# Block products seeded in PSUM, and two sums by accumulating DMA, in a cross-attention kernel

## The chip, the core and the metric

The kernel runs on one core of a Trainium2 chip. The core has TensorE (PE: matrix products into the accumulators in PSUM, with a weight load ahead of each that overlaps the product before), VectorE (DVE), ScalarE (ACT), GpSimd (POOL) and the queue of SyncE (SP). Transfers are issued by SP, ACT and POOL and carried by 16 DMA engines. Everything is fp32. The time is the device time of one launch in microseconds, the median of several runs.

## The reference

There are eight batches. For each, `x1` and `x2` are 512 x 1024:

```python
q = jnp.einsum('bcn,dc->bnd', x1, Wq) + bq
k = jnp.einsum('bcn,dc->bdn', x2, Wk) + bk[:, None]
v = jnp.einsum('bcn,dc->bdn', x2, Wv) + bv[:, None]
attn = jax.nn.softmax(jnp.einsum('bnd,bdm->bnm', q, k), axis=2)
attn_out = jnp.einsum('bcm,bnm->bcn', v, attn)
return attn_out + x1
```

with 64 rows in `Wq` and `Wk` and 512 in `Wv`.

## The kernel before

The values are not formed. For each batch the kernel computes y = x2 · E, where E holds the exponentials of the scores (1024 x 1024, keys by queries), scales the columns of y by the reciprocal sums, and then computes Wv · y, to which the bias and x1 are added. The first product is called stage "y", the second stage "o".

**Seven products instead of eight.** Both stages split their operands into 2 x 2 quarters ("11", "12", "21", "22") and use seven quarter products with sums of quarters: S1 to S4 on the left, T1 to T4 on the right. The table `MULT` names the operands of each product and the PSUM bank it goes to: products 1, 6, 5, 3 run on in the banks a0 and a1 (two halves j of 128 rows), products 2, 7, 4 in c0 and c1. Between products 1, 6 and 5 the running sum is copied out by ScalarE (L332) to tiles u1, u6, u5 in SBUF, and VectorE adds such a copy to bank c when a quarter of the result is evicted (`evict_y`, L502, `evict_o`, L548): `RESULT` says which copy goes with which quarter. The quarter "12" is bank a at the end, with no copy.

**A second level.** A quarter product of stage y is 8 matmuls of 128 x 128 by 128 x 512, or it is done "in blocks": its operands are split once more (`inner_left`, four sums of 128 x 256 each at L355; `inner_right`, four sums of 128 x 512 each at L367), and seven block products of two matmuls of 256 columns follow (`inner_product`, L374). Their partial products lie in PSUM tiles of the pool `ps_s`; ScalarE copies them to SBUF tiles d and v (L383), and VectorE adds those to the copies u or to the bank's content. Batch 0 has products 3 and 4 in blocks, batches 1 and 6 products 2, 3 and 4, batches 2 to 5 and 7 products 2, 3, 4 and 7 (`seven`, L712). Product 2 has a routine of its own, `multiply_2` (L388), with six VectorE additions (L418); `multiply_7` (L464) adds its d to u5 and u6 (L471).

**Sums.** S1, S2, S4 are VectorE additions of 128 x 1024 (`sum_a`, L110), S3 too, in place of "21". T1, T2, T3 are VectorE subtractions (`sum_e`, L262), T3 in place of "12". From batch 2 on, T4 is made by two ScalarE copies (L278) and two accumulating transfers (L280), issued by GpSimd.

**The order of work.** The order of each engine's queue is the order of the program text; only waits are added. `period` (L708) writes out one batch `s`, with the next batch `n` woven in: products 1, 2, 6 of y; scores of the first half of the queries of `n` (L191, copied by ScalarE, L200 and L198); the queries of the batch after it; products 5, 7, 3; scores of the second half; keys of the batch after; product 4; then stage o in the order 1, 6, 2, 5, 7, 3, 4. GpSimd finds the maxima and the sums over partitions by all-reduce (`highest` L221, `total` L226), issues the small transfers that turn a sum into a row of reciprocals (`shares`), adds up the exponentials by accumulating transfers (L555), and adds x1 to the results likewise (L551). SP loads `a` (x2 transposed, L133) and `x` (L126) and stores the results (L552).

Around the change in stage o stand these lines:

```python
        second(7)
        if s.b and n:
            sum_a(n, "S1", "S2")
        evict_o(s, "22")
        ...
            sum_a(n, "S3")
            inner_left(n, 2, n.a["12"], "aS4")
            inner_right(n, 2, n.e[0][:, 1], "eT4")
            second(3)
            evict_o(s, "12")
            second(4)
            evict_o(s, "21")
```

Tiles are named by tags, and a tag with one buffer makes a new tile wait for all uses of the old one. yT1, yT2 and yT4 hold T1, T2 and T4 of stage o, and lend themselves to sums of blocks in stage y; u1, y11, y12, y22, i2, aS4, eT1, eT2 likewise have several users.

## Time and profile before

| | |
|---|---|
| runs, median (lowest to highest of 3) | 690.9 us (690.63 to 691.11) |
| profiled execution, span from first to last instruction | 689.5 us |
| granted TensorE clock, mean | 0.999 |
| period of batch 3 (288.16 to 371.82) | 83.66 us; PE 83.66, DVE 80.06, ACT 35.64, POOL 24.72 busy; DMA share 0.67 |
| period of batch 7 (617.0 to 689.5) | 72.50 us; PE 68.82, DVE 59.73, ACT 15.69, POOL 9.42 busy; DMA share 0.46 |
| DMA queues | GpSimd's (q0) 36.25 MB, 30.1% of 16 engines' span; SP's (q1) 70.13 MB, 29.4% |
| T4's accumulating transfers | 12 of 512 KB, 6.8 us from issue to landing (median; 5.3 to 8.3) |

A row of the groups reads: line, engine, operation, output and inputs by the program's names, shapes, count, busy time in all, mean ns of one, and the idle time before with what ended it. Some rows that bear on the change:

```profile
L332 ACT COPY uy<-ps_ya 128x512 f32<-128x512 f32 x48 | 28.0, 586 | 138.9 <-PE ps_ya L321 124.9
L383 ACT COPY d<-ps_i 128x256 f32<-128x256 f32 x84 | 29.3, 374 | 47.6 <-PE ps_i L374 47.0
L548 DVE SCALAR_TENSOR_TENSOR uo<-ps_oc,bv_sb,uo 128x512 f32<-128x512 f32 x42 | 29.5, 741 | 1.6 <-PE ps_oc L321 1.6
```

A matmul of the program is two instructions in the profile, and matmuls overlap, so the mean of one is longer than the time it adds; the chain of waits shows what a group adds.

### The profile page before, as it was taken

To read this page: it belongs to the slowest core of one execution; us is meant where nothing else is said; L and a number is where in the kernel's file an instruction comes from. 1 tells how busy PE (TensorE), PEld (TensorE's weight loads), DVE (VectorE), ACT (ScalarE), POOL (GpSimd) and SP (SyncE) were. 2 spreads that over 40 slices of the span, in tenths; PEclk is the share of its full clock that TensorE was granted. 3 is DMA by queue.
4 is the path that set the end of the run, shared out by engine and by line. 5 is a ranking of instruction groups with operands and counts; after the bars stand their busy time and mean duration, and the time that the engine had idled before them with its cause. 6 is when DMAs were issued, how large, how long until landed. Compare 5 with 4: busy or idle time off the path is not lost.

```text
span 689.5 us, 6656 instructions
## 1 busy us (share of the span) xinstructions
PE 683.1 (99%) x2252; PEld 365.3 (53%) x2252; DVE 630.4 (91%) x809; ACT 275.7 (40%) x439; POOL 189.3 (27%) x147
## 2 busy tenths in 40 slices
PE   9999999999999999999999999999999999999997
PEld 5333554535545465455654566454754545545763
DVE  1999999988999889998999989999899988999894
ACT  2734263146233562435533454324544245333220
POOL 0124113521423123231232321423223241324100
PEclk9999999999999999999999999999999999999999
DMA  9666266954558854696638867298642874259403
GB/s 301 263 218 231 70 183 120 252 162 92 184 106 208 236 100 160 129 243 182 125 130 160 241 176 166 69 187 224 181 81 41 185 200 77 62 108 248 102 0 123
DMA packets 44723, 109.05 MB, mean 158 GB/s; under 512 B 4880, under 2 KB 7184, under 8 KB 44688
## 3 DMA queue, kind: packets, MB, share of 16 engines
q0 software_dynamic: 17424, 36.25, 30.1%
q1 hardware_dynamic: 25856, 70.13, 29.4%
q10 hardware_dynamic: 1408, 2.23, 1.1%
q8 instruction: 18, 0.29, 0.2%
q14 instruction: 17, 0.14, 0.1%
HBM read 72.62 MB, written 16.81 MB: 130 GB/s over the span
## 4 chain that ended last, share of the span: by engine, by line
PE 94%; DMA 3%; SPq 1%; ACT 1%; DVE 1%; issue 0%; DVEq 0%
PE ps_ya L321 24%; PE ps_i L374 17%; PE ps_oa L321 16%; PE ps_oc L321 12%; PE ps_s L191 6%; PE ps_yc L374 5%; PE ps_q L149 4%; PE ps_k L149 3%; PE ps_ya L374 3%; PE ps_yc L321 3%; DMA a<-in_x2T_dram 1%; DMA x_in_x_dram<-in_x_dram 1%; DMA x_head<-in_x_dram 1%; PE ps_sc L191 1%; PE ps_sa L191 1%; DVE aS L110 0%
## 5 line engine op out<-in xcount | busy, mean ns | idle before, releaser
L321 PE MATMUL ps_ya<-eT,aS 128*128 128x512 f32 x256 | 113.1, 595 | 0.0
L332 ACT COPY uy<-ps_ya 128x512 f32<-128x512 f32 x48 | 28.0, 586 | 138.9 <-PE ps_ya L321 124.9
L321 PEld LDWEIGHTS ps_ya<-eT,aS 128*128 128x128 f32 x256 | 48.0, 190 | 60.9 <-issue 58.8
L253 ACT ACTIVATE e<-e 128x1024 f32<-128x1024 f32 x60 | 63.0, 1059 | 42.3 <-DVE e L249 40.8
L249 DVE TENSOR_TENSOR e<-e,top 128x1024 f32<-128x1024 f32 x60 | 69.8, 1214 | 11.0 <-POOL top L221 11.0
L221 POOL PARTITION_ALL_REDUCE top<-max x16 | 32.8, 2052 | 154.6 <-DVE max L215 79.3
L226 POOL PARTITION_ALL_REDUCE den<-sum x16 | 59.2, 3701 | 40.8 <-DVE sum L215 35.8
L321 PE MATMUL ps_oa<-yT,w_S 128*128 128x512 f32 x128 | 57.6, 593 | 0.0
L321 PE MATMUL ps_oc<-y,w 128*128 128x512 f32 x128 | 57.6, 593 | 0.0
L321 PE MATMUL ps_ya<-e,a 128*128 128x512 f32 x128 | 56.3, 593 | 0.3 <-ACT e L244 0.3
L200 ACT COPY e<-ps_s 128x1024 f32<-128x1024 f32 x46 | 45.7, 1028 | 19.3 <-PE ps_s L191 18.1
L332 ACT COPY uo<-ps_oa 128x512 f32<-128x512 f32 x48 | 27.4, 583 | 53.0 <-PE ps_oa L321 41.3
L383 ACT COPY d<-ps_i 128x256 f32<-128x256 f32 x84 | 29.3, 374 | 47.6 <-PE ps_i L374 47.0
L551 POOL DMA_DIRECT2D uo<-in_x_dram x21 | 24.9, 1184 | 85.0 <-DVE uo L548 85.0
L191 PE MATMUL ps_s<-q,k 64*128 64x512 f32 x188 | 47.3, 608 | 0.8 <-ACT q L590 0.8
L555 POOL DMA_DIRECT2D sum<-e x21 | 25.7, 1222 | 66.5 <-DMA sum<-e 32.7
L321 PEld LDWEIGHTS ps_ya<-e,a 128*128 128x128 f32 x128 | 24.2, 190 | 31.3 <-issue 29.6
L321 PEld LDWEIGHTS ps_oa<-yT,w_S 128*128 128x128 f32 x128 | 24.2, 190 | 30.8 <-issue 29.9
L321 PEld LDWEIGHTS ps_oc<-y,w 128*128 128x128 f32 x128 | 24.0, 190 | 31.0 <-issue 28.5
L211 DVE TENSOR_TENSOR max<-max,e 128x1024 f32<-128x1024 f32 x30 | 36.7, 1225 | 3.0
L507 DVE TENSOR_TENSOR y<-y,den 128x512 f32<-128x512 f32 x54 | 33.7, 681 | 0.0
L548 DVE SCALAR_TENSOR_TENSOR uo<-ps_oc,bv_sb,uo 128x512 f32<-128x512 f32 x42 | 29.5, 741 | 1.6 <-PE ps_oc L321 1.6
(142 smaller groups left out, 1274.5 us busy)
## 6 DMA issues: line engine op xcount, KB each, us to landing
x_in_x_dram<-in_x_dram SPq DMA_DIRECT2D x60, 512.0 KB, 6.2
a<-in_x2T_dram SPq DMA_DIRECT2D x32, 512.0 KB, 6.3
sum<-e POOLq DMA_DIRECT2D x21, 512.0 KB, 5.1
uo<-in_x_dram POOLq DMA_DIRECT2D x21, 512.0 KB, 6.4
out_dram<-uo SPq DMA_DIRECT2D x21, 512.0 KB, 4.1
eT<-eT POOLq DMA_DIRECT2D x12, 512.0 KB, 6.8
den<-row POOLq DMA_DIRECT2D x16, 256.0 KB, 3.6
r<-in_x_dram POOLq DMA_DIRECT2D x7, 512.0 KB, 8.7
```

The costliest lines, as they stand in the source:

```text
L149: nc.tensor.matmul(ps[r, :], w_sb[:, c, :], s.x[:, c, ts(h, H)], start=(c == 0), stop=(c == CT - 1),)
L191: nc.tensor.matmul(ps[g], s.k[r, ts(i, P)], s.q[r, ts(h, H)], start=True, stop=True)
L200: nc.scalar.copy(e[:, :, i, :], whole)
L211: nc.vector.tensor_tensor(f, e[:, :, 0, :] if i == 1 else f, e[:, :, i, :], op)
L221: nc.gpsimd.partition_all_reduce(s.top[h], s.mx[h][:, 0, :], P, ReduceOp.max)
L226: nc.gpsimd.partition_all_reduce(s.den[h], s.mx[h][:, 0, :], P, ReduceOp.add)
L249: nc.vector.tensor_tensor(e, e, top, ALU.subtract)
L253: nc.scalar.activation(e, e, AF.Exp)
L321: nc.tensor.matmul(ps[:, n], left[ka][:, k, ts(j, P)], right[kb][:, k, n], start=opens and k == 0, stop=i in (2, 3, 4) and k == n_k - 1, s ...
L332: nc.scalar.copy(s.tmp[i][:, j, :], ps)
L374: nc.tensor.matmul(ps, s.inner[i][ka][:, k, :], s.inner[i, "t"][kb][:, k, :], start=opens and k == 0, stop=z in (2, 3, 4) and k == MH // 2 ...
L507: nc.vector.tensor_tensor(y[:, j, :], y[:, j, :], rden, ALU.mult)
```

## The change

In batches 2 to 7 (`late`) product 1 of y is done in blocks too, by a new routine `multiply_seeded`, which also takes over product 2 (batches 1 to 7) and product 7 (where it was in blocks). In this routine ScalarE copies a partial block product from the PSUM tile of `ps_s` to the place in bank a or c where it belongs, and later block products are accumulated onto it by matmuls there; one VectorE addition in PSUM (`complete`) follows. `multiply_2`, `inner_bank` and `multiply_7` go, and with them their additions. The blocks' sums for product 1 of the next batch are made in stage o, around the sums S1 and S2. The copies u1 of product 1 are made by hooks within product 2.

In stage o of all batches product 1 goes to a PSUM tile `both`, ScalarE copies it to a0 and a1, where product 6 runs on, and product 2 is accumulated onto `both`, which then is block 11 of the result; it is evicted by ScalarE with the bias (in the last batch by VectorE).

T3 of batches 2 to 7 is made by ScalarE, which negates "12", and accumulating transfers that add "22". S4 is loaded as "12" of x2 transposed and S2 is added by an accumulating transfer. Several sums of blocks move to other places in the order, and the scaling of y11, y22 and y12 with them.

```diff
+    def sum_t3(s, i):
+        t3 = s.t["T3"][:, i : i + 2, :]
+        nc.scalar.mul(t3, t3, -1.0)
+        nc.gpsimd.dma_start(t3, s.t["22"][:, i : i + 2, :], accum_op=ALU.add)
+
+    def sum_s4(s):
+        s.a["S4"] = sb.tile([P, MH, C // 2], F32, tag="aS4", name=f"aS4_{s.b}")
+        nc.sync.dma_start(s.a["S4"], x2T[s.b, 0, 1])
+        nc.gpsimd.dma_start(s.a["S4"], s.a["S2"], accum_op=ALU.add)
+
+    def copy_u1(s, j):
+        if j == 0:
+            s.tmp[1] = sb.tile([P, 2, H], F32, tag="u1", name=f"uy1_{s.b}")
+        nc.scalar.copy(s.tmp[1][:, j, :], s.bank["a", j])
...
+    def multiply_o1(s):
+        both = ps_s.tile([P, 2, H], F32, tag="sc", name=f"ps_o1_{s.b}")
+        for j in range(2):
+            s.bank["p", j] = ps = both[:, j, :]
+            for k in range(2):
+                nc.tensor.matmul(
+                    ps, w["11"][:, k, ts(j, P)], s.y["11"][:, k, :], start=k == 0, stop=False, skip_group_check=True
+                )
+            s.bank["a", j] = a = ps_a.tile([P, H], F32, tag=f"a{j}", name=f"ps_oa{j}_{s.b}_1")
+            nc.scalar.copy(a, ps)
...
+    def multiply_seeded(s, i, v_tag, hooks={}):
+        bank = MULT[i][2]
+        b0, b1 = (
+            ps_a.tile([P, H], F32, tag=f"{bank}{j}", name=f"ps_y{bank}{j}_{s.b}_{i}") for j in range(2)
+        )
+        s.bank[bank, 0], s.bank[bank, 1] = b0, b1
+        parts = ps_s.tile([P, 2, H], F32, tag="sc", name=f"ps_i{i}_{s.b}")
+        chain, third = parts[:, 0, left], parts[:, 1, left]
+        v = sb.tile([P, 2, H], F32, tag=v_tag, name=f"v{i}_{s.b}")[:, 0, left]
+        for z, ps, opens, out, of in (
+            (1, chain, True, b0[:, left], chain),
+            (7, third, True, v, third),
+            (6, chain, False, b1[:, left], chain),
+            (2, b0[:, left], False, None, None),
+            (5, chain, False, b0[:, right], chain),
+            (4, b1[:, left], False, b1[:, right], chain),
+            (3, b0[:, right], False, None, None),
         ):
+            inner_product(s, i, z, ps, opens)
+            if out is not None:
+                nc.scalar.copy(out, of)
+            if z in hooks:
+                hooks[z]()
+        def complete():
+            b = b1.rearrange("p (a n) -> p a n", a=2)
+            nc.vector.tensor_tensor(b, b, v.unsqueeze(1).to_broadcast([P, 2, H // 2]), ALU.add)
...
-        bank, add = RESULT[k]
+        bank, add = RESULT[k] if k != "11" else ("p", None)
...
-        seven = 2 <= s.b < B - 2 or n is None
+        late = s.b >= 2
+        seven = late and (s.b < B - 2 or n is None)
...
-        first(1)
+        if late:
+            complete_1 = multiply_seeded(s, 1, "y11")
...
+        if late:
+            shares(s, 0)
+            for i in range(1, MH):
+                fold(s, 1, i, "sum", ALU.add)
+            complete_1()
         sum_e(s, "T1", "T2")
-        if s.b < 2:
+        if late:
+            total(s, 1)
...
-            evict = multiply_2(s)
-            sums(s, 1)
-            evict()
+            complete_2 = multiply_seeded(
+                s, 2, "y22", {6: lambda: copy_u1(s, 0), 5: lambda: copy_u1(s, 1)} if late else {},
+            )
+            if late:
+                sum_t3(s, 0)
+                sum_t3(s, 2)
...
+            complete_2()
+            evict_y(s, "11", (1,))
...
             sum_t4(s)
-            sum_a(s, "S4")
-        sum_e(s, "T3")
+            if late:
+                sum_s4(s)
...
+        if late:
+            inner_left(s, 4, s.a["22"], "a12")
+            evict_y(s, "11", (2,))
...
         shares(s, 1)
         if seven:
+            inner_right(s, 7, s.t["T3"], "yT1", "yT2")
...
             first(5, (lambda: exponential(n, 0, 0)) if n else None)
+            inner_left(s, 3, s.a["S4"], "aI3")
             inner_right(s, 3, s.t["22"], "eT1")
-            inner_left(s, 4, s.a["22"], "a12")
-            add_7 = multiply_7(s, hooks[0])
-            add_7()
+            complete_7 = multiply_seeded(s, 7, "y12", hooks[0])
+            complete_7()
+            evict_y(s, "22", (1,))
             evict_3 = multiply_3(s, hooks[1])
-            evict_y(s, "22", (1,))
-            if n:
-                evict_3()
             inner_right(s, 4, s.t["T4"], "eT2")
-            if not n:
-                evict_3()
+            evict_y(s, "22", (2,))
+            evict_3()
+            evict_y(s, "12", (2,))
...
         if s.b and n:
+            inner_right(n, 1, n.e[0][:, 0], "yT1", "yT2")
             sum_a(n, "S1", "S2")
+            inner_left(n, 1, n.a["11"], "i2")
         evict_o(s, "22")
```

More of the change, by code (lines that the diff above doesn't have):

```diff
@@ L312, in multiply @@
         ka, kb, bank, opens = MULT[i]
+        if stage == "o" and i == 2:
+            bank, opens = "p", False
         for j in range(2):
@@ L383, in inner_product @@
             nc.scalar.copy(copy, ps)
-    def inner_bank(s, i, z):
-        return ps_s.tile([P, 2, H], F32, tag="sc", name=f"ps_i{i}{z}_{s.b}")[:, 0, left]
-    def multiply_2(s):
-        chain = ps_a.tile([P, H // 2], F32, tag="c0", name=f"ps_i20_{s.b}")
-        second = ps_a.tile([P, H // 2], F32, tag="c1", name=f"ps_i21_{s.b}")
-        third = inner_bank(s, 2, 2)
-        uv = sb.tile([P, 4, H // 2], F32, tag="i2", name=f"i2_{s.b}")
-        u, v = uv[:, 0:2], uv[:, 2:4]
-        for z, ps, opens, *copies in (
-            (1, chain, True, v[:, 0, :]),
-            (2, second, True),
-            (6, chain, False, u[:, 0, :]),
-            (7, third, True, v[:, 1, :]),
-            (5, chain, False, u[:, 1, :]),
-            (4, third, False),
-            (3, chain, False),
-        ):
-            inner_product(s, 2, z, ps, opens, *copies)
-        def evict():
-            u0, u1 = s.tmp[1][:, 0, :], s.tmp[1][:, 1, :]
-            s.y["11"] = y = sb.tile([P, 2, H], F32, tag="y11", name=f"y11_{s.b}")
-            for out, x, z in (
-                (u0[:, left], u0[:, left], v[:, 0, :]),
-                (y[:, 0, left], second, u0[:, left]),
-                (u1, u1, u.rearrange("p a n -> p (a n)")),
-                (y[:, 1, right], v[:, 1, :], u1[:, right]),
-                (y[:, 1, left], third, u1[:, left]),
-                (y[:, 0, right], chain, u0[:, right]),
-            ):
-                nc.vector.tensor_tensor(out, x, z, ALU.add)
-        return evict
@@ new lines, in multiply_seeded @@
+    def multiply_seeded(s, i, v_tag, hooks={}):
[15 more added lines that the diff above has]
+            (3, b0[:, right], False, None, None),
+        ):
+            inner_product(s, i, z, ps, opens)
[6 more added lines that the diff above has]
+            nc.vector.tensor_tensor(b, b, v.unsqueeze(1).to_broadcast([P, 2, H // 2]), ALU.add)
+        return complete
@@ L422, in multiply_onto @@
     def multiply_onto(s, i, d_tag, v_tag, hooks={}):
-        bank, opens = MULT[i][2:]
-        if opens:
-            for j in range(2):
-                s.bank[bank, j] = ps_a.tile([P, H], F32, tag=f"{bank}{j}", name=f"ps_y{bank}{j}_{s.b}_{i}")
+        bank = MULT[i][2]
         b0, b1 = (s.bank[bank, j] for j in range(2))
-        chain, third = inner_bank(s, i, 0), inner_bank(s, i, 2)
+        parts = ps_s.tile([P, 2, H], F32, tag="sc", name=f"ps_i{i}_{s.b}")
+        chain, third = parts[:, 0, left], parts[:, 1, left]
@@ L439, in multiply_onto @@
             6: (chain, False, d[:, 1, 0, :]),
-            2: (b0[:, left], opens),
+            2: (b0[:, left], False),
             5: (chain, False, d[:, 0, 1, :], d[:, 1, 1, :]),
-            4: (b1[:, left], opens),
+            4: (b1[:, left], False),
             3: (b0[:, right], False),
         }
-        for z in (1, 2, 7, 6, 4, 5, 3) if opens else (1, 7, 6, 2, 5, 4, 3):
+        for z in (1, 7, 6, 2, 5, 4, 3):
             inner_product(s, i, z, *steps[z])
@@ L462, in multiply_4 @@
             nc.vector.tensor_tensor(u6, u6, d[:, j, :], ALU.add)
-    def multiply_7(s, hooks):
-        d, complete = multiply_onto(s, 7, "i2", "y12", hooks)
-        def add():
-            complete()
-            for k in (5, 6):
-                nc.vector.tensor_tensor(s.tmp[k], s.tmp[k], d, ALU.add)
-        return add
     def multiply_3(s, hooks):
@@ L496, in evict_y @@
         y = s.y[k]
-        alone = 7 in s.inner and add in (5, 6)
         for step in steps:
@@ L500, in evict_y @@
                 if step == 1:
-                    ps, n = s.bank[bank, j], left if alone and j else slice(0, H)
-                    nc.vector.tensor_tensor(y[:, j, n], ps[:, n], s.tmp[add][:, j, n], ALU.add)
-                elif alone and j:
-                    for x, n in ((y, left), (s.tmp[add], right)):
-                        nc.vector.tensor_tensor(y[:, j, n], x[:, j, n], rden[:, n], ALU.mult)
+                    nc.vector.tensor_tensor(y[:, j, :], s.bank[bank, j], s.tmp[add][:, j, :], ALU.add)
                 else:
@@ L519, in bias @@
             return bv_sb[:, 2 * r + j : 2 * r + j + 1]
+        if s.b == B - 1 and k == "11":
+            o = s.x[:, 0:2, ts(h, H)]
+            for j in range(2):
+                nc.vector.scalar_tensor_tensor(
+                    o[:, j, :], s.bank[bank, j], bias(j), o[:, j, :], ALU.add, ALU.add
+                )
+                nc.sync.dma_start(out[s.b, ts(j, P), ts(h, H)], o[:, j, :])
+            return
         if s.b == B - 1 and add is None:
@@ L541, in evict_o @@
         if add is None:
-            o = sb.tile([P, 2, H], F32, tag="r", name=f"r_{s.b}")
+            o = sb.tile([P, 2, H], F32, tag="u1" if k == "11" else "r", name=f"r{k}_{s.b}")
             for j in range(2):
@@ L717, in second @@
         def second(i):
-            multiply(s, "o", i, w, s.y, 2, n is None and i == 3)
+            if i == 1:
+                multiply_o1(s)
+            else:
+                multiply(s, "o", i, w, s.y, 2, n is None and i == 3)
         open_t(s)
@@ L722, in period @@
             load_x(s, x1)
-        first(1)
+        if late:
+            complete_1 = multiply_seeded(s, 1, "y11")
+        else:
+            first(1)
         if s.b == 0:
             head_second(s, n)
+        if late:
[3 more added lines that the diff above has]
+            complete_1()
         sum_e(s, "T1", "T2")
-        if s.b < 2:
+        if late:
+            total(s, 1)
+        else:
             total(s, 0)
-        else:
-            shares(s, 0)
         if n:
@@ L740, in period @@
             shares(s, 0)
+            sum_e(s, "T3")
         else:
-            evict = multiply_2(s)
-            sums(s, 1)
-            evict()
+            complete_2 = multiply_seeded(
+                s,
+                2,
+                "y22",
+                {6: lambda: copy_u1(s, 0), 5: lambda: copy_u1(s, 1)} if late else {},
+            )
+            if late:
+                sum_t3(s, 0)
+                sum_t3(s, 2)
+            else:
+                sums(s, 1)
+            complete_2()
+            evict_y(s, "11", (1,))
             if s.b == 1:
@@ L747, in period @@
             sum_t4(s)
-            sum_a(s, "S4")
-        sum_e(s, "T3")
+            if late:
+                sum_s4(s)
+            else:
+                sum_a(s, "S4")
+                sum_e(s, "T3")
         if n:
@@ L754, in period @@
             inner_right(s, 4, s.t["T4"], "eT2")
-        if s.b:
             inner_left(s, 3, s.a["S4"], "aI3")
-        if s.b > 1 and not seven:
-            inner_left(s, 4, s.a["22"], "a12")
         if seven:
             inner_left(s, 7, s.a["S3"], "yT4")
-            inner_right(s, 7, s.t["T3"], "yT1", "yT2")
+        if late:
+            inner_left(s, 4, s.a["22"], "a12")
+            evict_y(s, "11", (2,))
         def add_exponential(i):
@@ L799, in period @@
             first(5, (lambda: exponential(n, 0, 0)) if n else None)
+            inner_left(s, 3, s.a["S4"], "aI3")
             inner_right(s, 3, s.t["22"], "eT1")
-            inner_left(s, 4, s.a["22"], "a12")
-            add_7 = multiply_7(s, hooks[0])
-            add_7()
+            complete_7 = multiply_seeded(s, 7, "y12", hooks[0])
+            complete_7()
+            evict_y(s, "22", (1,))
             evict_3 = multiply_3(s, hooks[1])
-            evict_y(s, "22", (1,))
-            if n:
-                evict_3()
             inner_right(s, 4, s.t["T4"], "eT2")
-            if not n:
-                evict_3()
+            evict_y(s, "22", (2,))
+            evict_3()
+            evict_y(s, "12", (2,))
         else:
@@ L820, in period @@
                 start_sum(n, 0)
+                if late:
+                    inner_left(s, 3, s.a["S4"], "aI3")
                 inner_right(s, 3, s.t["22"], "eT1")
@@ L831, in period @@
                 evict_y(s, "22", (1,))
-        for k in ("11", "12", "22"):
-            evict_y(s, k, (2,))
+            for k in ("12", "22") if late else ("11", "12", "22"):
+                evict_y(s, k, (2,))
         if s.b == 1:
```

## The prediction, made before the changed kernel ran

> Times called t count from the first product matmul of the fourth batch's period (288.16 us into the span), the steady state taken as the pattern. Periods are numbered by batch, 0 to 7.

> **What bounds it now.** I read the header, then the chain of waits, then a timeline of each engine over one period, then windows of 1.5 us for the DMA engines.

> ```profile
> span 689.5 us, 6656 instructions
> PE 683.1 (99%) x2252; PEld 365.3 (53%) x2252; DVE 630.4 (91%) x809; ACT 275.7 (40%) x439; POOL 189.3 (27%) x147
> PE 94%; DMA 3%; SPq 1%; ACT 1%; DVE 1%; issue 0%; DVEq 0%
> ```
> TensorE has no idle time to win back after the head; time can fall only by fewer matmul columns, and any wait put on TensorE shows in full. The chain prices a product:

> ```profile
> 288.16 6.87 PE ps_ya L321 x16
> 295.02 6.04 PE ps_i L374 x28
> ```
> A whole product of y takes 6.87 us (0.43 per instruction), one in seven blocks 6.04 (0.216 each, 0.863 per block product).

> VectorE is the second engine to know: its timeline in that period runs without gaps but for 1.83 us before the exponentials' subtraction and 0.49 us in product 3.

> ```profile
> 284.09 1.22 DVE L110 TENSOR_TENSOR a<-a,a 128x1024 f32<-128x1024 f32 x1
> 285.23 0.42 DVE L355 TENSOR_TENSOR aI<-a 128x256 f32<-128x256 f32 x1
> ...
> 286.69 0.68 DVE L367 TENSOR_TENSOR eI2eT<-e 128x512 f32<-128x512 f32 x1
> 287.41 0.69 DVE L367 TENSOR_TENSOR eI2eT<-eI2eT,e 128x512 f32<-128x512 f32 x1
> 288.02 0.68 DVE L367 TENSOR_TENSOR eI2eT<-e 128x512 f32<-128x512 f32 x1
> 288.62 0.68 DVE L367 TENSOR_TENSOR eI2eT<-e,eI2eT 128x512 f32<-128x512 f32 x1
> 289.22 1.40 DVE L548 SCALAR_TENSOR_TENSOR uo<-ps_oc,bv_sb,uo 128x512 f32<-128x512 f32 x2
> ```
> Start to start, four left sums take 1.46 us (285.23 to 286.69), four right sums 2.53 (to 289.22).

> **TensorE's work.** Product 1 of y goes into blocks for batches 2 to 7: 6 x (6.87 - 6.04) = **5.0 us less**. Products 2 and 7 were in blocks already where they are now; the block 11 of the result keeps its matmuls. So 690.9 - 5.0 = 685.9 is the floor. The sum is made against the span, 689.5; the 1.4 us outside it, up to the median of 690.9, are taken as unchanged.

> **ScalarE.** Per period: five block copies in product 1, one more in product 2 (L383: 0.372 us each), two negations for T3 (as L278's copy, 1.043), two bias copies for block 11 (L544: 0.687); 2.2 + 2.1 + 1.4 = 5.7 us on an engine that is busy 35.6 of 83.66 us. TensorE now waits for these copies: a block product that adds onto a copy comes one block product later, so 0.863 us covers 0.372 plus 0.04 from matmul end to copy start (the copies at L383 start so). No row has a copy that ends in PSUM. From below it costs no less than nothing of the end, being hidden; from above, at twice its row to SBUF (0.74), it still fits. Product 1 of the result: a 0.585 copy of the first half has the second half, 1.72 us, as cover. I take 0 for all of these. If ScalarE were late instead, as behind the wait of L332 for an output transfer (305.09, t = 16.9), about 1 us a period would be lost: the eviction of block 21 ends at t = 2.4 now and at about 3.3 then, its output goes out that much later, and the copies of the scores follow it, with 3 us to spare before and about 1 after.

> [...]

> **VectorE, in sum.** Per period it loses T3 (2.27 us), S4 (1.21 when undisturbed), two additions in product 7 (2.28), block 11's eviction (1.32) and trades product 2's eviction (2.6) for 1.9; it gains the right and left sums of product 1 (2.53 + 1.46) and one addition (0.65). About 3 us less in all, worth nothing by itself, since TensorE is the bound. What counts is order, at two places.

> **Place one: block 22's eviction in the result stage.** The sums for the next batch's product 1 are queued ahead of evict_o("22"). Their first writes tile yT1, which product 5 of the result reads until it ends; product 4 adds onto the bank that the eviction reads. In between TensorE has products 7 and 3: 6.87 us, or 6.69 from product 5's last end to product 4's first start (277.84 to 284.53). VectorE in that time: right sums 2.53, S1 and S2 2.39 (280.38 to 282.77), left sums 1.46, first half of the eviction 0.74: 7.12 us, plus 0.06 to start and 0.13 to the matmul. TensorE waits 7.31 - 6.69 = **0.62 us** in batches 2 to 5, where VectorE arrives about 1 us before product 5 ends. In batch 1 it arrives 0.25 late by its timeline (0.85 us), in batch 6 some 0.6 late, without the keys' cover (1.2 us). Sum 4 x 0.62 + 0.85 + 1.2 = **4.5 us lost**: nearly all of the gain. Bounds: 3 to 7.

> **Place two: T3 and S4 come by DMA.** Each period adds two transfers of 512 KB for T3, a load and an accumulation of 512 KB for S4. GpSimd issues them in the order T3, T3, T4, T4, S4 after the all-reduce of the denominators (3.18 us, now from about t = 13.3), at some 1.1 us each: T3 from t = 17.4, S4 at 21.7. Ahead of them on the engines are an output and now four loads, not three. Rows of the windows (engine times, clock, DMA share, GB/s at the end):

> ```profile
> 309.00:310.50 1.50, 1.50 (x8) 0.60 (x8) 1.47 (x5) 1.39 (x2) 0.00 (x0) 1.00 1.03 214
> 310.50:312.00 1.50, 1.50 (x10) 0.41 (x8) 1.47 (x5) 1.50 (x4) 0.00 (x0) 1.00 1.10 216
> 312.00:313.50 1.50, 1.50 (x10) 0.56 (x8) 1.50 (x3) 0.93 (x2) 0.00 (x0) 1.00 0.99 197
> 313.50:315.00 1.50, 1.50 (x8) 0.29 (x4) 1.45 (x2) 0.00 (x0) 0.00 (x0) 1.00 0.23 44
> ...
> 316.50:318.00 1.50, 1.50 (x5) 0.74 (x4) 1.47 (x2) 0.09 (x1) 0.00 (x0) 1.00 0.97 328
> ```
> T4's two accumulations run at 209 GB/s with the engines full: 1.05 MB in 5.0 us. They end at 313.5 (t = 25.3); the four loads of x that follow the queries' matmuls take 316.5 to 324 at 298 GB/s, 7.0 us for 2.1 MB. So the engines are full from before T4 to t = 36, but for 2.6 us. After the change T3 stands in T4's place and lands, behind one more load (1.8 us at 298 GB/s), at t = 27; T4 and S4's accumulation, 7.5 us of engine time, then meet the loads of x, 7.0 us, from the same t = 27. S4 lands at 34.5 if GpSimd's queue goes first, at 41.5 if SP's does. No row has both queues deep at once; I take the middle, **38**.

> [...]

> What waits for S4: product 3 of y in blocks. Its second block product, nominally at t = 40.15, needs left sums (1.46), three right sums (1.93) and 0.13: S4 by 36.6. At 38 TensorE waits 1.4 us. VectorE is held meanwhile with the completion of product 7, block 22, the right sums of product 4 and block 12 behind it, 8.3 us from there to the bank that the next scores' third pair needs, which TensorE reaches in 7.1: another 1.2. So **2.6 us a period** (0 to 6.1) in batches 2 to 5: **10.4 us** (0 to 24). Batch 6 has no load of x then, and a whole product 7 as cover: 0. Batch 7 has no scores and no queries between its products: product 7 starts at t = 25.8, its second block product at 26.7 needs three right sums after T3's landing at 27: 2.3 us; S4 at 34.5 holds product 3 by 38 - 35 = 3: **5 us** (0 to 8). GpSimd's small transfers for the shares stand behind S4 too; the shares are needed only after the sums that S4 holds, so 0.

> T3 itself in batches 2 to 5: its sums come before the subtraction that the exponentials need, which moves from 1.83 us of waiting to about 1 us of slack. A landing at 27 costs nothing, one after 28.5 would hold TensorE through ScalarE's queue.

> **Sum:** 690.9 - 5.0 + 4.5 + 10.4 + 5 = 705.8, so **706 us**; with each bound at its end 689 to 725, of which I keep 688 to 718.

> **Rivals.** (1) The transfers keep up: S4 before t = 36.6, as it would with GpSimd's queue served first (34.5). For it: the engines' share over the period is only 0.67. Against it: the windows above. Time 690.9 - 5.0 + 4.5 + 1 = 691.4, **not slower** in a measurable way. Chance 0.18. (2) The vector queue isn't the limit at block 22 either, because product 1's right sums start before product 5 ends or the sums overlap more; this decides from 0.6 us less VectorE time there. For it: VectorE has 3 us less to do. Against it: the tile yT1 and the order in the code. Time 685.9 to 688.5, **faster**. Chance 0.15. (3) The change doesn't do what it says: a ScalarE copy into PSUM takes over 0.82 us and every block chain waits for it; at 1.0 us, three waits of 0.2 in each of 18 products (six of 1, seven of 2, five of 7), 11 us on top of the 690.4 of floor and place one, about 701. Nothing in the rows speaks for it; 0.04, on the forecast's side. The forecast has 0.63.

> Of 690.9 us 0.2% is 1.4, about what a measurement tells from no change. Rival 1 splits between no change (0.13) and slower (0.05): faster 0.15, same 0.13, slower 0.72.

> **What would show it.** L374 with 6.04 us for product 1 in the chain; ScalarE's PSUM copies at 0.37; a wait of TensorE's weight loads for L548's successor near the end of each period, 0.6 us; VectorE idle before the left sums of product 3 with the transfer named as releaser, followed by idle TensorE; a DMA share near 1 up to t = 42. If VectorE waits for no DMA there, the forecast's largest term is wrong; if TensorE's idle time at product 4 of the result is under 0.2 us, so is place one.

## The result, and the profile after

The changed kernel takes 754.0 us (752.3 to 757.8), against 691.0 for the kernel before: the ratio is 1.092, 95% interval 1.0892 to 1.0948. It is slower by 63 us, where 15 were forecast.

The header and the engines' busy times of the changed kernel:

```profile
span 751.8 us, 6875 instructions
...
PE 701.2 (93%) x2324; PEld 373.2 (50%) x2324; DVE 591.3 (79%) x788; ACT 306.3 (41%) x502; POOL 232.9 (31%) x165
```

TensorE is idle for 7% of a longer span. What it waits for is in the view of waits, here TensorE's own (line it waits in, what it waits for, us in total, times, longest us):

```profile
PE ps_i L405 <- ACT v L437: 8.3, 18, 0.5
PE ps_i L405 <- ACT v L414: 7.4, 16, 0.5
PE ps_o L361 <- ACT ps_oa L365: 6.4, 8, 1.6
PE ps_i L405 <- ACT d L414: 6.3, 13, 0.6
PE ps_i L405 <- ACT ps_yc L437: 4.9, 11, 0.4
PE ps_i L405 <- DVE eI3eT L398: 4.1, 3, 2.5
PE ps_i L405 <- ACT ps_ya L437: 3.0, 6, 0.5
PE ps_oc L340 <- DVE uo L563: 2.2, 6, 0.4
PE ps_i L405 <- DVE eI7yT L398: 1.7, 1, 1.7
```

Six of the nine rows name ScalarE, with 36.3 us and 72 waits; L437 and L414 are its copies out of a block product's accumulator, L365 the copy of product 1 of the result. The waits that the prediction priced highest, for S4 and T3 (10.4 and 5 us), are small: S4 (eI3eT) 4.1 us and T3 (eI7yT) 1.7. Place one (uo) has 2.2.

TensorE's timeline over product 2 of y in the fourth batch (start, length, and in brackets the idle time before and its releaser):

```profile
314.72 1.03 PE L405 MATMUL ps_i<-e,a 128*128 128x256 f32 x4
316.19 1.13 PE L405 MATMUL ps_i<-eI2eT,aI 128*128 128x256 f32 x4 [0.45 <-ACT ps_yc L437]
317.79 1.13 PE L405 MATMUL ps_i<-eI2eT,aI 128*128 128x256 f32 x4 [0.46 <-ACT v L437]
318.75 1.03 PE L405 MATMUL ps_yc<-e,a 128*128 128x256 f32 x4
...
322.21 7.03 PE L340 MATMUL ps_ya<-eT,aS 128*128 128x512 f32 x16
```

and ScalarE's over the same stretch:

```profile
315.79 0.36 ACT L437 COPY ps_yc<-ps_i 128x256 f32<-128x256 f32 x1 [1.37 <-PE ps_i L405]
317.36 0.37 ACT L437 COPY v<-ps_i 128x256 f32<-128x256 f32 x1 [1.22 <-PE ps_i L405]
```

The second block product (z = 7) starts 1.47 us after the first, not 0.863, right after ScalarE's copy of the first ends (315.79 + 0.36 = 316.15). The third (z = 6) starts after the copy of the second. Neither adds onto the copy that it waits for: z = 7 opens the accumulator `third`, which is the other half of the tile; z = 6 adds onto `chain`, which was copied one block product before. So the copy is not slow; it takes 0.36 us, as long as one to SBUF. The matmul waits for a copy of the *other* accumulator. The wait stands in the program: in the trace the first weight load of the waiting block product (316.19) waits on semaphore 114, which ScalarE's copies count up, and starts 0.04 us after the copy's end. Both are slices of one PSUM tile, `parts`, in the changed kernel, where the kernel before took one tile for each (`inner_bank`). The product takes 322.21 - 314.72 = 7.49 us instead of 6.04. That is 1.45 more in 34 products (product 1 in 6 batches, 2 in 7, 7 in 5, 3 and 4 in 8 each): 49 us. Product 1 of the result has the same form, two halves of one tile `both`: its second half starts 0.87 us late in most batches and 1.7 in the first, 7.8 in all. With place one (six gaps of 0.53) and the gaps at S4 and T3 (4.6 and 1.9) that is 66.8 us of the 67.3 by which the span of 751.8 exceeds the forecast's floor for it, 689.5 - 5.0. Some 2.5 us stand twice in this sum, since four of the gaps at S4 and T3 hold a wait for ScalarE too. About as much is left out: 1.5 us of half clock (0.50 granted from 709 to 711) after the last batch's wait for S4, and 0.1 us by which TensorE starts again more slowly after each of the 14 waits in the result stage (the longest matmul of product 1 there takes 0.697 us, the median one 0.592).

### The profile page after: what moved, and what is told of

Its sections match the earlier page's. It is cut to its first block, busy times and chain, and to the rows that moved or that the text cites. A ratio compares the mean times of both kernels' runs of the same rounds, so it can differ in the third digit from the quotient of the medians.

```text
span 751.8 us, 6875 instructions
## 1 busy us (share of the span) xinstructions
PE 701.2 (93%) x2324; PEld 373.2 (50%) x2324; DVE 591.3 (79%) x788; ACT 306.3 (41%) x502; POOL 232.9 (31%) x165
## 5 line engine op out<-in xcount | busy, mean ns | idle before, releaser
L226 POOL PARTITION_ALL_REDUCE den<-sum x16 | 87.1, 5444 | 57.3 <-DVE sum L215 52.3
L351 ACT COPY uy<-ps_ya 128x512 f32<-128x512 f32 x36 | 21.0, 588 | 73.3 <-PE ps_ya L340 72.4
L414 ACT COPY d<-ps_i 128x256 f32<-128x256 f32 x64 | 22.3, 375 | 58.5 <-PE ps_i L405 58.5
L514 DVE TENSOR_TENSOR y<-y,den 128x512 f32<-128x512 f32 x64 | 40.8, 685 | 6.1 <-DMA den<-row 5.9
L238 POOL DMA_DIRECT2D den<-row x16 | 9.0, 560 | 113.9 <-DMA row<-few 113.9
L566 POOL DMA_DIRECT2D uo<-in_x_dram x14 | 16.5, 1176 | 76.9 <-DVE uo L563 47.2
L405 PE MATMUL ps_i<-eI3eT,aI 128*128 128x256 f32 x96 | 27.6, 412 | 10.1 <-DVE eI3eT L398 4.1
L361 PE MATMUL ps_o<-y,w 128*128 128x512 f32 x64 | 30.9, 605 | 6.4 <-ACT ps_oa L365 6.4
L475 DVE TENSOR_TENSOR d<-d,v 128x512 f32<-128x512 f32 x16 | 11.2, 699 | 29.1 <-ACT d L414 29.1
L405 PE MATMUL ps_i<-eI4eT,aI 128*128 128x256 f32 x96 | 26.3, 396 | 7.8 <-ACT d L414 4.0
L351 ACT COPY uo<-ps_oa 128x512 f32<-128x512 f32 x32 | 18.7, 587 | 33.1 <-PE ps_oa L340 28.7
```

Of the source, the lines that this page charges most:

```text
L226: nc.gpsimd.partition_all_reduce(s.den[h], s.mx[h][:, 0, :], P, ReduceOp.add)
L351: nc.scalar.copy(s.tmp[i][:, j, :], ps)
L361: nc.tensor.matmul(ps, w["11"][:, k, ts(j, P)], s.y["11"][:, k, :], start=k == 0, stop=False, skip_group_check=True)
L405: nc.tensor.matmul(ps, s.inner[i][ka][:, k, :], s.inner[i, "t"][kb][:, k, :], start=opens and k == 0, stop=z in (2, 3, 4) and k == MH // 2 ...
L514: nc.vector.tensor_tensor(y[:, j, :], y[:, j, :], rden, ALU.mult)
```

## The experiments

Theory A: the shared PSUM tiles make TensorE wait, and this is most of the loss. Theory B: the transfers and VectorE are late, as predicted, and the waits shown for ScalarE stand where TensorE would have waited anyway. Times are medians, but for experiments 1 and 3, which are one run each.

**1. Accumulators apart, in the changed kernel** (and nothing else):

```diff
-        parts = ps_s.tile([P, 2, H], F32, tag="sc", name=f"ps_i{i}_{s.b}")
-        chain, third = parts[:, 0, left], parts[:, 1, left]
+        chain, third = (
+            ps_s.tile([P, 2, H], F32, tag="sc", name=f"ps_i{i}{z}_{s.b}")[:, 0, left] for z in (0, 2)
+        )
```

> The changed kernel, but the block products' chain and third partial lie in two PSUM tiles, as before the change. Theory A (two slices of one PSUM tile tie TensorE to ScalarE's copies): each of 34 block products goes from 7.5 us back to 6.04, some 45 us in all, of which the wait for S4 takes some 8 back because product 3 comes earlier: about 717 us (708 to 722). Rival B (the copies into PSUM are themselves on TensorE's path): products keep 7.5 us and the time stays near 754.

Measured: 740.0 us, between the two. The waits for ScalarE inside the block products were gone but for 0.2 us, and other waits had grown: those for S4 (eI3eT and aS) to 21.7 us. The second step shows them more plainly.

**2. Both halves of product 1 of the result apart too:**

```diff
-        both = ps_s.tile([P, 2, H], F32, tag="sc", name=f"ps_o1_{s.b}")
         for j in range(2):
-            s.bank["p", j] = ps = both[:, j, :]
+            s.bank["p", j] = ps = ps_s.tile([P, 2, H], F32, tag="sc", name=f"ps_o1{j}_{s.b}")[:, 0, :]
```

> As split_chain, and product 1 of the result writes its two halves to two PSUM tiles. Theory A: the 8 waits of about 0.97 us between its halves go as well, 7.8 us: about 709 us (700 to 715); then the forecast's own terms are all that is left, and the forecast said 706. Rival B: near 754.

Measured: 737.6 us, ratio to before 1.0663 (1.0616 to 1.0709). That is 29 us above the 709 expected. TensorE's waits in this kernel:

```profile
PE ps_i L404 <- DVE eI3eT L397: 13.8, 6, 2.5
PE ps_i L404 <- DMA aS<-aS: 8.1, 5, 2.6
PE ps_oc L340 <- DVE uo L564: 3.2, 6, 1.1
PE ps_i L404 <- DVE eI7yT L397: 2.9, 1, 2.9
PE ps_i L404 <- DMA e<-e: 2.3, 1, 2.3
```

With ScalarE out of the way, TensorE comes earlier to product 3, and S4's landing (aS) is now what it waits for. VectorE in the fourth batch:

```profile
336.15 0.43 DVE L385 TENSOR_TENSOR aI<-aS 128x256 f32<-128x256 f32 x1 [4.94 <-DMA aS<-aS]
```

The period begins at 296.43, so S4 lands at t = 39.7; predicted was 38. And each stall has an echo. Windows of the same kernel (length, busy us of PE, PEld, DVE, ACT, POOL with instructions, then TensorE's granted clock, DMA share and GB/s):

```profile
334.00:337.00 3.00, 2.69 (x13) 1.99 (x11) 0.81 (x3) 1.60 (x3) 0.00 (x0) 1.00 1.01 379
337.00:340.00 3.00, 0.52 (x3) 0.24 (x2) 2.96 (x7) 0.37 (x1) 1.80 (x2) 1.00 0.54 137
340.00:343.00 3.00, 3.00 (x10) 2.43 (x10) 2.96 (x6) 0.75 (x3) 0.00 (x0) 0.63 0.91 169
343.00:346.00 3.00, 3.00 (x13) 2.51 (x12) 2.89 (x6) 1.60 (x3) 1.19 (x1) 0.80 0.08 14
```

TensorE stands still in most of 337 to 340, and then works on at a granted clock of 0.63 and 0.80 as means of three microseconds (0.50 in each single one from 341 to 344): the stall is paid once more, in part, after it is over. This happens in six batches. Busy time weighed by the missing clock, in windows of 1 us, comes to about 12.6 us.

**3. The kernel before, with its accumulators put into one tile.** This is the opposite test: no transfer, no seed, no new order, only the tile.

```diff
-        chain, third = inner_bank(s, i, 0), inner_bank(s, i, 2)
+        parts = ps_s.tile([P, 2, H], F32, tag="sc", name=f"ps_i{i}_{s.b}")
+        chain, third = parts[:, 0, left], parts[:, 1, left]
```

> The kernel before with one edit: chain and third partial of products 3, 4 and 7 are two slices of one PSUM tile. No copy goes into PSUM here. Theory A: two waits (0.6 and 0.74 us) in each of 16 products 3 and 4, one of 0.74 in each of 5 products 7, whose order puts another block product between: 16 x 1.35 + 5 x 0.74 = 25 us slower, about 716 us. Rival B: no change, 691.

Measured: 718.5 us in one run, 27.5 above before. Its TensorE in products 7 and 3 of the fourth batch:

```profile
333.68 1.03 PE L374 MATMUL ps_i<-eI7yT,aI 128*128 128x256 f32 x4
335.17 1.13 PE L374 MATMUL ps_i<-eI7yT,aI 128*128 128x256 f32 x4 [0.46 <-ACT v L383]
...
338.73 1.03 PE L374 MATMUL ps_i<-e,aS 128*128 128x256 f32 x4
340.22 1.13 PE L374 MATMUL ps_i<-eI3eT,aI 128*128 128x256 f32 x4 [0.46 <-ACT d L383]
341.81 1.13 PE L374 MATMUL ps_i<-eI3eT,aI 128*128 128x256 f32 x4 [0.46 <-ACT v L383]
```

The same waits of 0.46 us. Product 7 has one here, since its order of blocks puts another block product between the first two, and takes 6.78 us; so 16 products at 1.45 and 5 at 0.74 make 27, as measured. Theory A holds for the tile.

**4. Block 22's eviction ahead of the left sums** (place one), on top of experiment 2:

```diff
-            inner_right(n, 1, n.e[0][:, 0], "yT1", "yT2")
             sum_a(n, "S1", "S2")
-            inner_left(n, 1, n.a["11"], "i2")
+            inner_right(n, 1, n.e[0][:, 0], "yT1", "yT2")
         evict_o(s, "22")
+        if s.b and n:
+            inner_left(n, 1, n.a["11"], "i2")
```

> As split_both, with S1 and S2 of the next batch before the right sums of product 1, then the eviction of block 22, then the left sums. The wait of product 4 of the result for that eviction (6 x 0.53 us in the changed kernel) should go: 3.2 us less than split_both. If TensorE waits elsewhere in its place, the difference is under 1 us.

Measured: 714.6 us, ratio 1.0337 (1.032 to 1.0354): 23.0 less than experiment 2, not 3.2. The wait for uo is gone, and the waits for S4 have fallen from 21.9 to 14.6 us (eI3eT 10.4, aS 4.2), with the clock falling in three places, not six. So place one and S4's lateness are coupled, and neither can be priced while the other is there. The next four kernels take them apart.

**5 to 8. S4, then T3 too, back on VectorE, with place one as it is and with block 22 first.** The core of the edit; its first part stands for S4 alone (5, 7), and all three parts for both (6, 8):

```diff
-            if late:
-                sum_s4(s)
-            else:
-                sum_a(s, "S4")
+            sum_a(s, "S4")
...
-            if late:
-                sum_t3(s, 0)
-                sum_t3(s, 2)
...
+            sum_e(s, "T3")
```

> The kernel after with its PSUM tiles apart (737.6 us) and S4 taken back from the accumulating transfer and formed by VectorE; T3 still comes by accumulating transfer. Theory A (what holds product 3, and with it the granted clock, is S4's late landing): the waits for S4, 14.8 + 8.9 us by gaps, and the lower clock after them go, and 737.6 falls to the floor of 685.9 plus place one (4) plus T3's wait in the last batch (2): about 692. Theory B (it is the queue of transfers as a whole: T3 and T4 land late too once product 1 is faster): only S4's 1 MB a period leaves the engines, and the time stays at 712 or more.

> As the run with S4 on VectorE, but T3 is formed by VectorE too, so no transfer is added by the change at all. Theory A (S4 was the wait, T3 costs little): the same time as with S4 alone on VectorE, within 2 us: 690. Theory B (the transfers in sum): clearly less than that run. Rival C (VectorE becomes the bound, with 3.5 us more work a period than in the kernel after): 700 or more, with TensorE waiting for left and right sums.

> S4 on VectorE, T3 by transfer, and the eviction of block 22 ahead of the inner left sums of the next product 1. If place one is its measured wait alone (0.53 to 0.7 us in six batches), it is 3 to 4 us under the run with S4 on VectorE: 688. If the 23 us that this reordering gave in the kernel with both transfers came through earlier transfers, no more than 4 us is to be had here; a difference of 10 or more would say that place one itself is worth far more than its wait.

> PSUM tiles apart, the eviction of block 22 ahead of the left sums, S4 and T3 both on VectorE: what is left of the change is product 1 of y in blocks, the seeds in PSUM and block 11 kept in PSUM. Theory A: the floor of 685.9 us and up to 1.5 us above it, so faster than before (690.9) by 0.5%. Rival C (VectorE is the bound now, or the ScalarE copies cost something after all): 691 or more.

Measured, all with the accumulators apart:

| S4 and T3 | order of the changed kernel | block 22 first | worth of the order |
|---|---|---|---|
| both by transfer | 737.6 | 714.6 | 23.0 |
| T3 by transfer, S4 on VectorE | 697.5 (ratio 1.0077 to 1.0106) | 690.9 (0.9982 to 1.0) | 6.6 |
| both on VectorE | 694.0 (1.0026 to 1.0054) | 687.7 (0.9937 to 0.9962) | 6.3 |

Read down, S4's transfer costs 40.1 us in the first column and 23.7 in the second; T3's costs 3.5 and 3.2. The expectation of 692 for S4 on VectorE was 5.5 too low, and that of 688 with block 22 first 2.9. Theory A holds: S4 was the wait, not the transfers in sum. T3 costs a little more than the 2 us supposed. Read across, place one is worth 6.3 to 6.6 without S4's lateness, more than its visible wait of 3.2. From start to start, the six gaps at product 4 of the result in the kernel with both sums on VectorE are 0.79 us in batch 1, 0.53 in batches 2 to 5 and 1.28 in batch 6, 4.2 in sum, and 4.8 with the 0.1 us to start again after each. One wait of 1.0 in product 7 of batch 4 and 0.8 more at a bank of the scores are most of the rest. The 23 us come largely through S4: with block 22 first, GpSimd issues S4's accumulation 1.0 to 2.5 us earlier in the period (batches 3 to 6), and it lands 1.4 to 3.8 us earlier.

The last kernel is faster than the one before: 687.7 us, ratio 0.995, interval 0.9937 to 0.9962. That is 1.8 above the floor, 0.3 more than expected; in the profiled execution 0.8 us of it is a wait for VectorE's y at a bank of the scores in batch 2, and 0.5 one for VectorE's T sums before product 6 in batch 7. Its page and TensorE's timeline over products 1 and 2 of the fourth batch:

```profile
span 686.1 us, 6854 instructions
...
PE 678.8 (99%) x2324; PEld 378.5 (55%) x2324; DVE 620.6 (90%) x806; ACT 294.7 (43%) x490; POOL 216.8 (32%) x147
```

```profile
288.24 1.03 PE L404 MATMUL ps_i<-e,a 128*128 128x256 f32 x4
289.10 1.89 PE L404 MATMUL ps_i<-eI1yT,aI 128*128 128x256 f32 x8
...
294.28 1.03 PE L404 MATMUL ps_i<-e,a 128*128 128x256 f32 x4
295.14 1.89 PE L404 MATMUL ps_i<-eI2eT,aI 128*128 128x256 f32 x8
```

Two products of 6.04 us with seeds in PSUM, the block products 0.86 apart and no idle time between them.

**9. The same kernel with the accumulators back as slices of one tile each** (the edits of 1 and 2 reversed):

> The kernel with all four mends (687.7 us), with the accumulators put back as after has them: chain and third partial as two slices of one PSUM tile, both halves of product 1 of the result as two slices of another. No added transfer, no place one. Theory A (the waits for ScalarE's copies through the shared tile are most of the loss, 1.46 us in each of 34 products and 7.8 us at product 1 of the result): 687.7 + 49.6 + 7.8 = 745. Rival (part of those waits only stands where the transfers would have held TensorE anyway): 725 or less.

Measured: 743.8 us (743.7 to 744.3), 56.1 above 687.7. Theory A again: the waits cost this with no transfer added, so they do not stand where late transfers would have held TensorE anyway.

**10. Only product 1 of the result back in one tile** (the edit of 2 reversed):

> The kernel with all four mends (687.7 us), with only product 1 of the result on two slices of one PSUM tile again. Theory A: 8 batches at 0.97 us, so 695.5. Rival: the wait is taken up by the wait at product 4 of the result, 6.9 us later, and nothing is lost: 688.

Measured: 695.6 us, 7.9 above 687.7; the other 48 of the 56 are the block products'.

**11. Product 1 of y whole:**

```diff
-            complete_1 = multiply_seeded(s, 1, "y11")
+            first(1)
...
-            complete_1()
```

> The kernel with all four mends (687.7 us), with product 1 of y computed whole in batches 2 to 7, so without seeds there; VectorE still makes the sums for its blocks, unused. If a block product is worth 6.87 - 6.04 us and the seeds cost nothing: 6 x 0.83 = 5.0 us slower, 692.7. If the seeds cost TensorE time: less than 5 us slower.

Measured: 691.5 us (690.6 to 692.2), 3.8 above 687.7. Product 1 takes 6.87 us there, and 6.04 above, as in the prediction. From the start of the second batch's period to the end the two profiled executions differ by 4.8 us, so the seeds cost TensorE next to nothing. The stretch before, in which both kernels run the same program, took 119.0 us here and 120.1 there, and the difference begins with the warm-up matmuls (4.6 against 5.5 us). So in these two executions the missing 1.2 of 5.0 lies almost wholly outside the change; for the other runs this isn't shown.

**12. S4 ahead of T4 in GpSimd's queue**, on top of experiment 4:

```diff
+            if late:
+                sum_s4(s)
             sum_t4(s)
-            if late:
-                sum_s4(s)
-            else:
+            if not late:
```

> The kernel with PSUM tiles apart and block 22 first (714.6 us, S4 and T3 by transfer), with S4's load and accumulation issued ahead of T4's two accumulations instead of behind them. Theory A (S4 costs what it does because it lands behind T4 in GpSimd's queue): T4's 1.05 MB at 209 GB/s are 5.0 us, S4 lands that much earlier and most of the 23.7 us that S4's transfer costs over VectorE's sum goes: about 695. Rival (the engines are full of loads in that stretch, so that the order in one queue moves S4 by little, or T4 is what comes late then): 705 or more.

Measured: 699.7 us, ratio 1.0123 (1.0091 to 1.0155): 14.9 of the 23.7 us are won back, between the two numbers. The issues of transfers, first in the kernel of experiment 4 (tile, queue, times, size, median us from issue to landing):

```profile
eT<-eT POOLq DMA_DIRECT2D x12, 512.0 KB, 13.9
aS<-aS POOLq DMA_DIRECT2D x6, 512.0 KB, 18.0
```

and then with S4 ahead:

```profile
eT<-eT POOLq DMA_DIRECT2D x12, 512.0 KB, 15.0
aS<-aS POOLq DMA_DIRECT2D x6, 512.0 KB, 10.3
```

S4 lands 7.7 us sooner after its issue, TensorE no longer waits for it, and VectorE does once, for 2.3 us; T4 pays 1.1. What is left is another wait: TensorE for a bank of the scores behind VectorE's y (L496, 4.4 us in two places) and T3 in the last batch (3.3). So S4's place in the queue is most of its price, not all.

## Why the prediction was wrong, step by step

- **ScalarE's copies, "I take 0 for all of these": this step failed,** and cost 56 of the 63 us, by the kernel in which nothing else is late (experiment 9). Mended first, with S4 and T3 still late, the same fault gives back only 16.4 (754.0 to 737.6). Its sum went by which block product *adds onto* a copy: 0.863 us of cover for a copy of 0.372. The copy's length was right (0.36), and so was the order of the block products. But the program's waits go by PSUM tile, as the tile alone shows (27.5 us in experiment 3, 56.1 in experiment 9), and the change had put two accumulators into one. So a block product that goes into that tile right behind a copy out of it waits for the copy with no cover at all, twice in each product. The working even priced two near things, a copy of up to 0.74 us and a third rival with slow copies; both took the copy's duration as the doubtful number, where the doubtful one was whose copy is waited for. The line that shows it, `parts[:, 0, left], parts[:, 1, left]` in place of two calls of `inner_bank`, was in the diff.
- **The floor, 5.0 us less for product 1:** right; the product's time is as worked out, 6.87 to 6.04, and the whole is worth 4.8 from the second batch on, 3.8 by the medians (experiment 11).
- **Place one, 4.5 us:** place and mechanism as predicted. In the changed kernel it is six waits that shift TensorE by 0.53 us, 3.2 in sum. Without the other losses they come to 0.79, four times 0.53, and 1.28 (experiment 6), against 0.85, four times 0.62, and 1.2 in the working, and their removal is worth 6.3.
- **Place two, 15.4 us:** this term failed too, by its size. The landing was predicted at t = 38. In the fourth batch it is 39.7 (experiment 2) and 40.3 (the changed kernel, issue at 330.12 plus 17.4, less the period's start of 307.18); over batches 2 to 5 it is 39.7 to 43.7 and 39.6 to 42.0. The 38 was an estimate, the middle between GpSimd's queue first (34.5) and SP's first (41.5); in which order the DMA engines serve the two was not shown. In the changed kernel the term shows only 6.5 us of gaps, some 2.5 of them waits for ScalarE too, since TensorE itself comes late to product 3: the unforeseen loss hid most of the foreseen one. Without it S4's and T3's transfers cost 43.6 us, above even the sum of its upper bounds, 24 + 8. Waits are 26.7 of it by the gaps, with batch 6 among them, which the working had at 0; some 12.6 are the lower clock after each stall, which no step had; 2.3 are a wait for T3's own transfer (e) in the last batch, and the last 2 are of the size of one wait in batch 4, told below. Of the 2.6 us a period, the 1.2 at the scores' bank do not show in experiment 2. T3 was predicted to land at t = 27, and does so at 28.1 to 31.7 in batches 2 to 5 of experiment 2. At 31.7, in batch 4, VectorE waits 2.30 us for it, ScalarE's exponentials come late after that, and TensorE waits 1.64 us for the copy behind them: the path that the working had named for a landing after 28.5. In the last batch TensorE waits for T3 at product 7, with 1.7 us in the changed kernel and 2.9 in experiment 2, against 2.3.
- **Rivals.** That the transfers keep up (0.18) and that the kernel is faster (0.15) fell. The latter's time, 685.9 to 688.5, is what the change gives with its tiles apart, block 22 first and both sums back on VectorE (687.7).

In this order the account closes: 687.7 for what is good in the change, 56.1 for the shared tiles, and 10.2 (743.8 to 754.0) for place one, S4 and T3, of which the trace shows 3.8 at product 4 of the result, 4.0 at S4 and T3 beyond the waits for ScalarE, and 1.5 of half clock.

## What to carry to other kernels

Before a copy beside matmuls is priced as hidden, look at which tile each lies in, not only which data it reads: if a second accumulator moved into the same tile as a slice, count a full copy and what TensorE loses around it at every change of engine (here 0.7 us a time for a copy of 0.36: two waits made 1.45). Price waits in the order in which they would stand, each without the others, because the first can hide the next: here 48 us of waits hid more than 30 us of late transfers, and mending only the first gave 14 us. A sum moved from an engine to an accumulating transfer is worth the engine's time only if that engine is the bound (with both sums on VectorE it is busy for 90% and TensorE for 99%); its landing depended here on what stood ahead in the same queue (18.0 us behind T4, 10.3 ahead of it).

## What the runs showed of the hardware

```profile
337.35:340.76 3.41, 0.97 (x5) 0.90 (x6) 3.38 (x8) 0.36 (x1) 1.50 (x2) 1.00 0.67 145
340.76:344.18 3.42, 3.42 (x10) 2.67 (x9) 3.38 (x7) 1.70 (x3) 0.15 (x1) 0.50 0.55 100
```

and then in experiment 1, where the wait falls into two windows (1.63 and 1.04 us idle) and the clock stays at 1.00:

```profile
609.73:613.15 3.42, 1.79 (x6) 0.68 (x4) 2.52 (x6) 0.95 (x2) 1.80 (x2) 1.00 0.22 50
613.15:616.56 3.41, 2.37 (x11) 2.14 (x12) 3.38 (x7) 0.74 (x2) 0.00 (x0) 1.00 0.97 180
616.56:619.97 3.41, 3.41 (x17) 2.64 (x17) 3.09 (x6) 0.65 (x3) 1.19 (x1) 1.00 0.18 31
```

A copy by ScalarE from PSUM to PSUM, 128 x 256 in fp32, took 0.36 us, no more than one to SBUF (0.37).
